# Layer 3 of a four-layer convolution kernel: a first copy in two parts, gate chains at other slots, scales of three tiles on VectorE

## The chip, the cores and the metric

The kernel runs as one program on one core of a Trainium2 chip. The metric is the device time of one execution in microseconds (us). A core has five engines that run side by side, each with its own queue, in order: TensorE (PE: matrix products; PEld is its weight load), VectorE (DVE), ScalarE (ACT), GpSimd (POOL) and SyncE (SP, which here only issues DMAs). An instruction whose inputs or buffers aren't ready waits, and all that stands behind it in its engine's queue waits too.

## The reference

The kernel computes four layers on x of 4 x 256 x 48 x 48 floats, each `x = x + layer(groupnorm(x))`: attention (layer 0), a gated multiplication (1), a non-local block with a batch norm (2), and layer 3, the one that is changed:

```python
x = x + _L3_conv_ref(_gn(x), attn_w1, attn_w2, refine_w, refine_b)
...
def _L3_conv_ref(x, attn_w1, attn_w2, refine_w, refine_b):
    p = jnp.mean(xw, axis=(2, 3))
    h = jax.nn.leaky_relu(p @ attn_w1.T, SLOPE)
    a = jax.nn.sigmoid(h @ attn_w2.T)
    y = xw * a[:, :, None, None]
    y = conv_general_dilated(y, refine_w, padding='SAME', feature_group_count=C)
    y = y + refine_b[None, :, None, None]
    mu, var = mean(y), mean(square(y - mu))       # per sample and channel
    return leaky_relu((y - mu) * rsqrt(var + EPS), SLOPE)
```

`_gn` is a group norm with 32 groups of 8 channels; `refine_w` is a 3 x 3 depthwise kernel, one per channel; SLOPE is 0.01.

## The kernel before

Layers 0 to 2 (and their long run of products) are left as they are by the change. Layer 3 takes the last 150 us. Its work is cut into 8 tiles: 4 samples (`n`) by 2 halves of the channels (`k`), a tile being 128 channels by 48 x 48 pixels. The last sample's tiles are 6 and 7. The order of the samples is `SEQ`.

**Making a tile's image.** Layer 2's last product and the batch norm are applied on the way: `w_product` (L1650, PE) makes a chunk, `grow` (L1712, DVE) scales it, adds x and writes it into a padded image `pad` of 50 x 50 (five buffers), `border` (L1721, L1724, POOL) fills the rim with the value that the group norm turns to zero, `square` (L1736, ACT) sums squares for the group norm.

**Shifted copies.** The depthwise convolution runs on PE. For each half image (26 padded rows of 50 columns) 32 channels at a time are copied into `shifted`, at up to four shifts, so that one product contracts over several taps: 12 pieces `(j, q)` of 32 partitions by `CL` = 1298 columns, in one of three buffers `sh`. `place` (L1748 to L1756) makes a copy by SP's DMA (L1750), ACT (L1752), POOL (L1754) or DVE (L1756). Of later tiles, 8 pieces go by SP (`spread_out`) and 4 by ACT and DVE (`keep_here`). The two halves of tile 0 have a list of their own in `spread_first`.

**The convolution.** A tile is 6 *slots*, 48 in all. A slot (`products`, L1883) is 8 rows of the output: 3 row offsets by 4 groups of 32 channels, 12 products. Two slots fill one PSUM tile `cv`, one of three *groups* `g` of 768 pixels. ACT evicts it into `x` with its sum (`evict`, L1895), and sums its squares (`square`, L1906).

**The gate chain.** The gate `a` and the group norm of a sample are folded into one scale per channel, `rsa`, which is only needed after the convolution. Each sample has a chain of eight steps, which run at the slots `GATE_AT`, counted from the first slot of the sample's first tile:

1. `total` (L1795 to L1798, POOL) -> `gn_sq`
2. `groups` (L1802, PE), the sum over groups of channels
3. `read` (L1806, ACT) and `inverse` (L1810, L184, L1814, POOL) -> `pm`
4. `first_layer` (L1819, PE) on `pm`
5. `hidden` (L1826, ACT)
6. `leaky` (L1831, DVE) -> `hl`
7. `second_layer` (L1836, PE) on `hl`
8. `gate` (L1843, ACT) and `scaled` (L1847 to L1852, POOL) -> `rsa`

**The end of a tile.** When all groups are evicted: `moments` (L1915 to L1922, six small operations), `scales` (L1940 to L1958, of which the reciprocal root, L184, is always on POOL), `shift` (L1964, L1966), then per group `scale` (L1972, ACT), `leak` (L1978, DVE), `gain` (L1983, DVE: adds the residual) and `store` (L2016, SP). Of the last tile the sums come from `stats` and `aggregate` (L1928, L1932, DVE) on PSUM itself. A group's residual can also be added by PE with the identity as weights: `keep_up` and `join` (L1998, with ACT's L2010 behind it). `judge` is a check on layer 0's sums, whose last step `compare` (L2042, DVE) writes one number that the host reads.

**The order.** Each engine's order is the order of the calls (`manual_schedule`). `put_tile`, `put_before` and `put_chain` enter the calls into `events` with a slot and a rank; the slots are run in order, and in a slot the calls go by rank, calls of one rank in the order in which they were entered (tile 5's before the last sample's chain, for one). The ranks, from first to last: FRONT, CONV, PRODUCT, GROW, MID, EVICT, SMALL, MOMENTS, SQUARE, SCALE, LAST, PLACE, STORE. Behind slot 47 stands a tail written out by hand.

Of the kernel before, what the change touches and what calls it, by code (L numbers as in the profile page):

```python
# [23 lines left out]
NSL = N // SL  # L24
# [54 lines left out]
def usual_path(  # L79
    tc, x, wqkv, wout, vecs, dww, thphi_w, thphi_b, g_w, g_b, W_w, attn_w1, attn_w2, refine_w, out  # L80
):
    nc = tc.nc
    B = x.shape[0]
# [113 lines left out]
    def hum(out, n):  # L197

        for _ in range(n):
            nc.tensor.matmul(out, lhsT=gmat, rhs=gmat, start=True, stop=True)  # L200
# [798 lines left out]
    def strips_pe(b, norm, res):  # L999
# [103 lines left out]
        while n < len(rounds):  # L1103
            add()
            u = rounds[n][0]
            if u in placed and seen >= placed[u] + SETTLED and clock["t"] not in taken:
                product(n)
                n += 1
                if n + 1 < len(rounds):
                    build(n + 1)  # L1110
            for _ in range(FILLS_AT_ONCE):
                if not left or not may_fill(left[0][0], n):
                    break
                v, c = left.pop(0)
                place(v, c)
                if c == 15:
                    placed[v] = seen
            seen += 1
            yield 1
# [385 lines left out]
    for b in range(B):  # L1505
# [12 lines left out]
        if b + 1 < B:  # L1518
# [8 lines left out]
            at = [s for s in range(n) if s in work or s % NG == AT_TOTAL]  # L1527
# [76 lines left out]
    w_all = ps_w.tile([P, 2, 512], F32, name="w3")  # L1604
# [6 lines left out]
    def g_tile():  # L1611

        return cv_last["ps"][:, 1, SL:]
# [12 lines left out]
    W2 = HW + 2  # L1626
    NG3 = NSL // 2
    GW = 2 * SL
    RS = SL // HW
    HB = HW // 2  # L1630
    CH = (HB + 2) * W2
    CL = CH - 2
    NPAD = 5
    pads = [lp.tile([P, W2 * W2], F32, tag=f"pad{i}", name=f"pad{i}") for i in range(NPAD)]
    shifted = [lp.tile([P, 4, CH], F32, tag=f"sh{i}", name=f"sh{i}") for i in range(3)]
# [106 lines left out]

    HELD = [96, 96, P, P]

    def place(i, h, j, q, how):
        to = shifted[(2 * i + h) % 3][32 * q : 32 * q + 32, j, :CL]
        c0 = h * HB * W2 + SHIFT[j, q]
        fr = pads[i % NPAD][32 * j : 32 * j + 32, c0 : c0 + CL]  # L1748
        if how == "sp":
            nc.sync.dma_start(to, fr)  # L1750
        elif how == "act":
            nc.scalar.copy(to, fr)  # L1752
        elif how == "pool":
            nc.gpsimd.tensor_copy(to, fr)  # L1754
        else:
            nc.vector.tensor_copy(to, fr)  # L1756
# [3 lines left out]
    def spread_out(i, h):  # L1760

        for j, q in AWAY:
            place(i, h, j, q, "sp")

    def keep_here(i, h, js, how):

        for j in js:
            place(i, h, j, j, how)

    def spread_first(h):  # L1770

        if h == 0:
            how = dict(zip(AWAY, ("sp", "sp", "sp", "sp", "sp", "sp", "dve", "pool")))
            how |= {(0, 0): "act", (1, 1): "act", (2, 2): "act", (3, 3): "pool"}
        else:
            how = dict.fromkeys(AWAY, "sp")
            how |= {(0, 0): "dve", (1, 1): "pool", (2, 2): "dve", (3, 3): "pool"}
        for (j, q), e in how.items():
            place(0, h, j, q, e)

    class Chain:

# [239 lines left out]
    def judge():  # L2022

        of = {}

        def lows():
            ok = lp.tile([P, 2, LW], F32, name="ok")
            nc.vector.tensor_scalar(ok[:, 0, :], lsum, SUM_HI, None, ALU.is_le)
            nc.vector.tensor_scalar(ok[:, 1, :], lmin, SUM_LO, None, ALU.is_ge)
            of["okm"] = lp.tile([P, 1], F32, name="okm")  # L2030
            nc.vector.tensor_reduce(of["okm"], ok, AX.XY, ALU.min)

        def count():
            of["ps"] = g_tile()[0:1, 0:1]
            nc.tensor.matmul(of["ps"], lhsT=of["okm"], rhs=ones[:, 0:1], start=True, stop=True)

        def read():
            of["n"] = lp.tile([1, 1], F32, name="sound_n")
            nc.scalar.copy(of["n"], of["ps"])

        def compare():
            nc.vector.tensor_scalar(sound, of["n"], P - 0.5, None, ALU.is_ge)  # L2042

        return [(0, MID, lows), (2, SMALL, count), (3, MOMENTS, read), (5, MID, compare)]

    GATE_AT = {
        0: (3, 5, 6, 9, 10, 11, 11, 12), B - 1: (-2, -1, 0, 3, 4, 5, 7, 8),
    }
    for n in range(1, B - 1):
        GATE_AT[n] = (-2, 1, 2, 5, 6, 7, 9, 10)  # L2050
    chains = [Chain(n) for n in range(B)]
    convs = [Conv(i) for i in range(len(TILES))]

# [5 lines left out]
    grow(0, L2C - 1, first[L2C - 1], [0])  # L2059
    grow(0, 0, first[0], [1])  # L2060
    spread_first(0)
    for c in range(1, L2C):
        grow(0, c, first[c], [1])
    centres()
    spread_first(1)
    for c in range(L2C):
        square(0, c)
# [7 lines left out]
    FRONT, CONV, PRODUCT, GROW, MID, EVICT, SMALL, MOMENTS, SQUARE = range(9)  # L2075
    SCALE, LAST, PLACE, STORE = range(9, 13)
    events = {}

    def at(t, rank, fn):
        events.setdefault(t, []).append((rank, fn))  # L2080
# [23 lines left out]
    def put_tile(i, t, cv, final):  # L2104
        for s in range(NSL):
            at(t + s, CONV, lambda s=s: cv.products(s))
        if final:
            for s in range(NSL - 1):
                at(t + s + 1, MOMENTS, lambda s=s: cv.stats(s))
            return  # L2110
        for g in range(NG3):
            at(t + 2 * g + 2, EVICT, lambda g=g: cv.evict(g))
            at(t + 2 * g + 3, SQUARE, lambda g=g: cv.square(g))
        at(t + 2, EVICT, cv.centre)
        soon = t + 2 * NSL == T
        t += 0 if soon else 1 if i == len(convs) - 3 else 3 if cv.k else 5 if t == 0 else 4
        if soon:
            at(t + 9, MOMENTS, lambda: cv.moments(nc.vector))
            at(t + 9, MOMENTS, lambda: cv.scales(nc.vector))
            at(t + 10, FRONT, lambda: cv.shift(nc.vector))  # L2120
            for g in range(NG3):
                at(t + 10, SCALE, lambda g=g: cv.scale(g))
            return
        at(t + 8, FRONT, lambda: cv.moments(nc.gpsimd))
        at(t + 8, MOMENTS, cv.scales)
        at(t + 8, LAST, cv.shift)
        for g in range(NG3):
            at(t + 9 + g, SCALE, lambda g=g: cv.scale(g))
            u = t + (10 if t == 5 else 11) + g
            at(u, LAST, lambda g=g: cv.leak(g))  # L2130
            at(u, LAST, lambda g=g: cv.gain(g))
            at(u + 1, STORE, lambda g=g: cv.store(g))
# [4 lines left out]
    T = len(convs) * NSL  # L2137
    for i, cv in enumerate(convs):
        t = i * NSL
        put_tile(i, t, cv, i == len(convs) - 1)  # L2140
        if i > 1:
            put_before(t, i)
        if i:
            for h in range(2):
                at(max(0, t - 6 + 3 * h), PLACE, lambda i=i, h=h: spread_out(i, h))
            for dt, h, js, how in HERE:
                at(t + dt, PLACE, lambda i=i, h=h, js=js, how=how: keep_here(i, h, js, how))
        if i % NK == 0:
            put_chain(t, chains[i // NK].steps())
        if i < NK:  # L2150
            at(t + 18, STORE, lambda k=cv.k: reload(k))
    put_chain(13, judge())
    for t in range(min(events), T):
        for _, fn in sorted(events.pop(t, ()), key=lambda job: job[0]):
            fn()
    cv = convs[-1]
    cv.stats(NSL - 1)
    cv.aggregate()
    cv.scales(nc.vector)
    was = convs[-2]  # L2160
    was.leak(0)
    cv.shift(nc.vector)
    for g in range(NG3):
        cv.scale(g, cv.ps[g])
    hum(w_all[:, 1, SL:], 12)
    was.keep_up(1, w_all)
    was.leak(1)
    was.join(1, w_all)
    was.keep_up(2, cv.ps[0])
    was.leak(2)  # L2170
    was.join(2, cv.ps[0])
    was.gain(0)
    was.store(0)
    was.store(1)
    for g in range(NG3 - 1):
        cv.leak(g)
        cv.gain(g)
        if g == 0:
            was.store(2)
        cv.store(g)  # L2180
    cv.leak(NG3 - 1)
    for h, eng in enumerate((nc.scalar, nc.sync)):
        cv.gain_half(NG3 - 1, h)
        eng.dma_start(
# [771 lines left out]
def kernel(tc, *args):  # L2956


    sound = usual_path(tc, *args)
    with tc.If(sound == 0):  # L2960
        general_path(tc, *args)
# [72 lines left out]
```

## Time and profile before

| what | value |
|---|---|
| median of 3 runs | 3460.08 us (3459.35 to 3461.13) |
| the profiled execution: its own time | 3461.47 us |
| the profiled execution: span, first to last instruction | 3459.7 us |
| granted TensorE clock, mean over the span | 0.996 |
| last 21.0 us (3438.70 to 3459.70), busy | PE 8.37, DVE 13.54, ACT 7.31, POOL 1.10 |
| convolution slots 36 to 47 (3412.10 to 3438.70), busy | PE 26.60 of 26.60, DVE 15.97, ACT 20.05, POOL 15.29 |
| the 25.43 us ahead of these (3386.67 to 3412.10), busy | PE 21.65, DVE 22.00, ACT 24.66, POOL 14.29 |

Times within the execution are counted from the span's start. In a row of a timeline the columns are the start, the busy time, the engine, the line, the operation with output and input tiles, its shape, the number of records merged into the row, and in brackets the idle time before it with the engine, tile and line (or DMA) that ended it. In the windows view a row gives a stretch, its length, the busy time and the instructions of PE, PEld, DVE, ACT and POOL, the granted clock (1.00 is full speed), the share of the DMA engines that were busy, and GB/s. The clock line of the page is in tenths, one digit for each of 40 equal slices of the span.

### The profile page before, as it was taken

To read this page: it belongs to the slowest core of one execution; us is meant where nothing else is said; L and a number is where in the kernel's file an instruction comes from. 1 tells how busy PE (TensorE), PEld (TensorE's weight loads), DVE (VectorE), ACT (ScalarE), POOL (GpSimd) and SP (SyncE) were. 2 spreads that over 40 slices of the span, in tenths; PEclk is the share of its full clock that TensorE was granted. 3 is DMA by queue.
4 is the path that set the end of the run, shared out by engine and by line. 5 is a ranking of instruction groups with operands and counts; after the bars stand their busy time and mean duration, and the time that the engine had idled before them with its cause. 6 is when DMAs were issued, how large, how long until landed. Compare 5 with 4: busy or idle time off the path is not lost. (4 is left out here: it accounts for less than half of the span.)

```text
span 3459.7 us, 88715 instructions
## 1 busy us (share of the span) xinstructions
PE 3397.6 (98%) x37678; PEld 1711.7 (49%) x37678; DVE 2540.6 (73%) x3298; ACT 2297.1 (66%) x3690; POOL 824.9 (24%) x734
## 2 busy tenths in 40 slices
PE   8999999999999999999999999999999999899988
PEld 5555545555545444545454445554544444445533
DVE  3455545568788788687888787878887878857777
ACT  5565556565886687557866875568758855444577
POOL 2433333320011011101110010111011105776434
PEclk9999999999999999999999999999999999999999
DMA  2211111111111111121111110111111110221067
GB/s 91 49 23 27 22 27 22 27 22 27 21 32 22 27 22 27 27 72 22 27 22 27 15 31 15 31 18 31 18 28 17 30 21 9 59 62 11 8 152 230
DMA packets 111590, 127.20 MB, mean 37 GB/s; under 512 B 42912, under 2 KB 101648, under 8 KB 110416
## 3 DMA queue, kind: packets, MB, share of 16 engines
q1 hardware_dynamic: 109936, 119.53, 17.1%
q8 instruction: 297, 4.87, 0.6%
q10 hardware_dynamic: 1248, 1.91, 0.2%
q14 instruction: 109, 0.89, 0.1%
HBM read 56.99 MB, written 11.80 MB: 20 GB/s over the span
## 5 line engine op out<-in xcount | busy, mean ns | idle before, releaser
L330 ACT ACTIVATE pt<-sc 128x768 f32<-128x768 f32 x1944 | 1473.4, 810 | 759.8 <-PE sc L324 753.3
L370 DVE TENSOR_TENSOR acc<-acc,pt 128x768 f32<-128x768 f32 x1368 | 1367.1, 999 | 145.5 <-ACT pt L330 51.8
L344 PE MATMUL av<-pt,v 64*64 64x384 f32 x13824 | 1274.9, 484 | 0.0
L324 PE MATMUL sc<-q,k 64*64 64x384 f32 x13824 | 1270.1, 482 | 0.5 <-ACT pt L330 0.5
L324 PEld LDWEIGHTS sc<-q,k 64*64 64x64 f32 x13824 | 525.4, 133 | 589.6 <-issue 556.5
L344 PEld LDWEIGHTS av<-pt,v 64*64 64x64 f32 x13824 | 518.2, 133 | 568.4 <-issue 521.5
L421 POOL TENSOR_TENSOR o<-o,rinv 128x384 f32<-128x384 f32 x95 | 120.3, 1267 | 1712.4 <-DMA rinv<-rinv 1702.4
L355 POOL TENSOR_TENSOR half<-pt 128x768 f32<-128x768 f32 x189 | 369.0, 1957 | 495.2 <-ACT pt L330 417.0
L739 DVE SCALAR_TENSOR_TENSOR x<-pj,bo,x 128x384 f32<-128x384 f32 x192 | 118.5, 617 | 346.3 <-ACT row L388 188.0
L951 ACT ACTIVATE prod<-pd,wt 128x256 f32<-128x256 f32 x486 | 340.7, 761 | 0.2
L370 DVE TENSOR_TENSOR acc<-acc,half 128x768 f32<-128x768 f32 x171 | 187.6, 1097 | 169.4 <-POOL half L355 168.2
L625 PE MATMUL pj<-xs,w 128*128 128x384 f32 (+1 forms) x720 | 275.4, 505 | 0.0
L625 PEld LDWEIGHTS pj<-xs,w 128*128 128x128 f32 x720 | 124.1, 189 | 127.9 <-ACT v L664 34.3
L974 DVE TENSOR_REDUCE prod<-prod 128x256 f32<-128x1280 f32 x114 | 168.7, 1480 | 0.9 <-ACT prod L951 0.9
L344 PE MATMUL av<-pt,qv 64*64 64x384 f32 x1728 | 169.0, 495 | 0.0
L324 PE MATMUL sc<-qv,kd 64*64 64x384 f32 x1728 | 165.3, 487 | 2.3 <-ACT pt L330 2.2
L723 PE MATMUL pj<-o,wo 128*128 128x384 f32 (+1 forms) x384 | 161.3, 502 | 1.1 <-DVE x L739 0.8
L364 DVE TENSOR_TENSOR acc<-pt 128x768 f32<-128x768 f32 x99 | 119.7, 1209 | 39.3 <-ACT pt L330 39.1
L659 PEld LDWEIGHTS pj<-w,xs 128*128 128x128 f32 x1080 | 134.4, 191 | 24.2 <-issue 1.2
L659 PE MATMUL pj<-w,xs 128*128 128x128 f32 x1080 | 134.9, 275 | 0.0
L417 POOL TENSOR_TENSOR o<-raw 128x384 f32<-128x384 f32 x95 | 120.8, 1271 | 45.9 <-ACT raw L413 44.7
L413 ACT COPY raw<-av 128x768 f32<-128x768 f32 x108 | 86.4, 800 | 48.3 <-PE av L344 47.8
(304 smaller groups left out, 2256.4 us busy)
## 6 DMA issues: line engine op xcount, KB each, us to landing
xs<-in_x_dram SPq DMA_DIRECT2D x90, 384.0 KB
sh<-pad SPq DMA_DIRECT2D x126, 162.2 KB
rinv<-rinv SPq DMA_DIRECT2D x208, 94.5 KB
out_dram<-x SPq DMA_DIRECT2D x23, 384.0 KB
w<-in_wqkv_dram SPq DMA_DIRECT2D x32, 192.0 KB
x<-in_x_dram SPq DMA_DIRECT2D x4, 1152.0 KB
x<-in_x_dram SPq DMA_DIRECT2D x9, 384.0 KB
rinv<-ls SPq DMA_DIRECT2D x208, 1.5 KB
```

Of the source, the lines that this page charges most:

```text
L324: nc.tensor.matmul(ps[c * D : (c + 1) * D, h, :SL], lhsT=u["of"]["k"][r, j0 : j0 + D], rhs=u["of"]["q"][r, u["qc"]], start=True, stop=True,)
L330: nc.scalar.activation(pt, ps[:, :, :SL], AF.Exp, scale=u["scale"])
L344: nc.tensor.matmul(u["av"][h * D : (h + 1) * D, half, :SL], lhsT=value(u, j, h)[r], rhs=pt[r, h, :], start=j == 0, stop=j == JB - 1,)
L355: nc.gpsimd.tensor_add(half, pts[0], pts[1])
L370: nc.vector.tensor_add(u["acc"], u["acc"], term)
L417: eng.tensor_add(u["sum"], u["raw"][:, 0, :], u["raw"][:, 1, :])
L421: eng.tensor_mul(o, o, u["rinv"])
L625: nc.tensor.matmul(ps[:, :n], lhsT=at["w"][:, k, t, :], rhs=xs[s][:, k, :n], start=k == 0, stop=k == NK - 1,)
L659: nc.tensor.matmul(ps[:, i * P : (i + 1) * P], lhsT=xs[s][:, k, i * P : (i + 1) * P], rhs=at["w"][:, k, 2, :], start=k == 0, stop=k == NK - 1,
L723: nc.tensor.matmul(ps[:, :n], lhsT=wo[:, p, k * P : (k + 1) * P], rhs=o["o"][:, :n], start=True, stop=True,)
L951: nc.scalar.activation(bufs[n % 3][:, :, min(n, 1) + i].rearrange("p (r c) -> p r c", c=AS), pd[:, PAD + dr : PAD + dr + AS, PAD + dc : PA ...
L974: nc.vector.tensor_reduce(to, bufs[n % 3][:, :, : min(n, 1) + len(taps)], AX.X, ALU.add)
```

## The change

1. The first half image of tile 0 is copied in two parts for all 12 pieces: the columns of the first 10 rows (`RS + 2`, 500 of 1298 columns, which slot 0 reads), then the rest. Each piece stays with its engine.
2. `compare` runs at slot 13 + 9, last of its slot, where it ran at 13 + 5.
3. The chains of the last two samples run at the slots (-2, 1, 2, 3, 4, 5, 5, 6). Before, the third sample (first slot 24) had (-2, 1, 2, 5, 6, 7, 9, 10), and the last one (first slot 36) (-2, -1, 0, 3, 4, 5, 7, 8).
4. Tiles 4, 5 and 6 get their moments, scales and shift on VectorE at `t + 8` (`t` is the tile's first slot); scales from `t + 9`, leaks and gains from `t + 11` (tile 6: two scales at `t + 9`, one at `t + 10`, leaks and gains from `t + 10`), each group's store a slot later. Before, tile 4 had them on GpSimd at `t + 12`, tile 5 at `t + 9`, and tile 6 on VectorE at `t + 9` and `t + 10` with its leaks, gains and stores in the tail.
5. In the tail only tile 7's first group is joined by PE; the two joins of tile 6 go, its last group's gain is on VectorE.

```diff
-    def place(i, h, j, q, how):
-        to = shifted[(2 * i + h) % 3][32 * q : 32 * q + 32, j, :CL]
+    def place(i, h, j, q, how, part=slice(0, CL)):
+        to = shifted[(2 * i + h) % 3][32 * q : 32 * q + 32, j, part]
         c0 = h * HB * W2 + SHIFT[j, q]
-        fr = pads[i % NPAD][32 * j : 32 * j + 32, c0 : c0 + CL]
+        fr = pads[i % NPAD][32 * j : 32 * j + 32, c0 + part.start : c0 + part.stop]
...
-        for (j, q), e in how.items():
-            place(0, h, j, q, e)
+        top = (RS + 2) * W2
+        for part in (slice(0, top), slice(top, CL)) if h == 0 else (slice(0, CL),):
+            for (j, q), e in how.items():
+                place(0, h, j, q, e, part)
...
-        return [(0, MID, lows), (2, SMALL, count), (3, MOMENTS, read), (5, MID, compare)]
+        return [(0, MID, lows), (2, SMALL, count), (3, MOMENTS, read), (9, LAST, compare)]
 
     GATE_AT = {
-        0: (3, 5, 6, 9, 10, 11, 11, 12), B - 1: (-2, -1, 0, 3, 4, 5, 7, 8),
+        0: (3, 5, 6, 9, 10, 11, 11, 12), B - 1: (-2, 1, 2, 3, 4, 5, 5, 6),
     }
     for n in range(1, B - 1):
         GATE_AT[n] = (-2, 1, 2, 5, 6, 7, 9, 10)
+    GATE_AT[B - 2] = GATE_AT[B - 1]
...
-        soon = t + 2 * NSL == T
-        t += 0 if soon else 1 if i == len(convs) - 3 else 3 if cv.k else 5 if t == 0 else 4
-        if soon:
-            at(t + 9, MOMENTS, lambda: cv.moments(nc.vector))
-            at(t + 9, MOMENTS, lambda: cv.scales(nc.vector))
-            at(t + 10, FRONT, lambda: cv.shift(nc.vector))
+        if i >= len(convs) - 4:
+            soon = i == len(convs) - 2
+            at(t + 8, MOMENTS, lambda: cv.moments(nc.vector))
+            at(t + 8, MOMENTS, lambda: cv.scales(nc.vector))
+            at(t + 8, LAST, lambda: cv.shift(nc.vector))
             for g in range(NG3):
-                at(t + 10, SCALE, lambda g=g: cv.scale(g))
+                at(t + 9 + g // (1 + soon), SCALE, lambda g=g: cv.scale(g))
+                u = t + 11 - soon + g
+                at(u, LAST, lambda g=g: cv.leak(g))
+                at(u, LAST, lambda g=g: cv.gain(g))
+                at(u + 1, STORE, lambda g=g: cv.store(g))
             return
+        t += 3 if cv.k else 5 if t == 0 else 4
...
-    was = convs[-2]
-    was.leak(0)
+    was.leak(NG3 - 1)
     cv.shift(nc.vector)
     for g in range(NG3):
         cv.scale(g, cv.ps[g])
     hum(w_all[:, 1, SL:], 12)
-    was.keep_up(1, w_all)
-    was.leak(1)
-    was.join(1, w_all)
-    was.keep_up(2, cv.ps[0])
-    was.leak(2)
-    was.join(2, cv.ps[0])
-    was.gain(0)
-    was.store(0)
-    was.store(1)
-    for g in range(NG3 - 1):
+    cv.keep_up(0, w_all)
+    was.gain(NG3 - 1)
+    was.store(NG3 - 2)
+    was.store(NG3 - 1)
+    for g in range(NG3):
         cv.leak(g)
-        cv.gain(g)
-        if g == 0:
-            was.store(2)
-        cv.store(g)
-    cv.leak(NG3 - 1)
+    cv.join(0, w_all)
+    cv.store(0)
+    cv.gain(1)
+    cv.store(1)
     for h, eng in enumerate((nc.scalar, nc.sync)):
         cv.gain_half(NG3 - 1, h)
```

More of the change, by code (lines that the diff above doesn't have):

```diff
@@ L2155, in usual_path @@
             fn()
-    cv = convs[-1]
+    cv, was = convs[-1], convs[-2]
     cv.stats(NSL - 1)
```

## The prediction

> **What bounds the kernel now.** I read the page first, then the timeline of single engines, then the granted clock of some stretches.
>
> ```profile
> span 3459.7 us, 88715 instructions
> PE 3397.6 (98%) x37678; PEld 1711.7 (49%) x37678; DVE 2540.6 (73%) x3298; ACT 2297.1 (66%) x3690; POOL 824.9 (24%) x734
> PEclk9999999999999999999999999999999999999999
> ```
>
> TensorE (PE) is busy 98% of the span, so a wait that PE is spared or given counts in full. All edits lie in the last 150 us (layer 3). There PE's timeline shows each wait in brackets; a slot of the convolution is 24 records of L1883 (12 f32 products, two records each) and lasts 2.0 us.
>
> ```profile
> 3311.25 0.80 PE L1883 MATMUL cv<-sh,taps 96*32 96x384 f32 x2 [1.03 <-DMA sh<-pad]
> 3312.69 4.43 PE L1883 MATMUL cv<-sh,taps 96*32 96x384 f32 x22 [0.64 <-DMA sh<-pad]
> ...
> 3386.67 6.01 PE L1883 MATMUL cv<-sh,taps 96*32 96x384 f32 x72
> 3392.61 0.39 PE L1819 MATMUL cv<-pm,w 128*64 128x1 f32 x4
> ...
> 3412.10 0.38 PE L1802 MATMUL cv<-gn_sq,gmat 128*128 128x2 f32 x2 [2.88 <-POOL gn_sq L1798]
> 3412.41 9.73 PE L1883 MATMUL cv<-sh,taps 96*32 96x384 f32 x96
> 3422.07 0.39 PE L1819 MATMUL cv<-pm,w 128*64 128x1 f32 x4
> 3422.40 7.95 PE L1883 MATMUL cv<-sh,taps 96*32 96x384 f32 x96
> ```
>
> Three waits stand there: 1.67 us for the first copies and 2.88 us at the last sample's L1802. Four slots after the latter took 9.73 us, four later ones 7.95: 1.78 us lost to the clock. The windows view has the granted clock in its last column but two (0.57; 0.50 in an earlier layer's stretch):
>
> ```profile
> 3412.00:3416.00 4.00, 3.90 (x26) 2.53 (x30) 2.49 (x3) 3.94 (x9) 2.74 (x7) 0.57 0.98 342
> 3173.60:3180.40 6.80, 6.53 (x42) 2.95 (x46) 2.57 (x10) 1.30 (x2) 1.40 (x1) 0.50 0.08 5
> ```
>
> The gate chain crosses all engines. What its L1819 waits for is `pm`, GpSimd's last step (L1814); VectorE (DVE), which the change loads more, has one hole in this part:
>
> ```profile
> 3391.16 0.95 POOL L1814 TENSOR_TENSOR pm<-dev,gn_rs 128x2 f32<-128x2 f32 x1
> 3410.30 4.27 DVE L1756 COPY sh<-pad 32x1298 f32<-32x1298 f32 x5
> 3421.85 0.96 DVE L1978 SCALAR_TENSOR_TENSOR x<-x 128x768 f32<-128x768 f32 x1 [7.27 <-ACT x L1972]
> ```
>
> **The change part by part.** Times are those of the profile of before.
>
> *First half image in two parts.* Twelve copies become 24 (SyncE 6 to 12 issues, ScalarE 3 to 6, DVE 1 to 2, GpSimd 2 to 4). SyncE issues every 0.64 us and a copy lands 2.6 to 3.1 us later, so the six first parts land about as early as the sixth whole one did or sooner, with 38% of the bytes (500 of 1298 columns). Slot 0 then has up to 1.67 us less to wait. But DVE runs without a gap to 3317.02 (L444) and idles only 0.97 us before the grow at 3317.99; PE's next product, L1650 at 3319.93, needs that grow's buffer. Hence no more than about 1.6 can be had. Twenty issues from 3306.89 end at 3319.0 and land near 3321.6, where slot 3 starts at 3322.0: just hidden, and a miss costs the same again. Bounds −2.1 (clock drop also shortened) and 0; I take −1.3.
>
> *Sound compare later.* One DVE instruction of 0.13 us, from slot 18 to slot 22, last of its slot. The 1.85 us that the waits view puts on it (L1650 at 3367.56) ends with the grow of 3366.37 to 3367.51, queued ahead of it. 0.
>
> *Sample three's chain (tiles 4 and 5).* L1802 and the read stay; L1819 moves from after slot 29 to after slot 27, L1836 from after 33 to after 29. PE reaches L1819 at 3386.67 + 1.98 = 3388.65. But `pm` is ready at 3392.11: ScalarE's read is at 3389.08, then GpSimd's 0.97, 0.72 and 0.95, and nothing makes them earlier. PE waits 3.5 (the two small-op prices on GpSimd, 0.2 and 0.95, allow 2.4). Slots 28 and 29 end near 3396.6; the hidden read (L1826) stands behind the eviction of 3396.46 to 3397.48, so L1831 follows at 3397.75, L1836 at 3397.85: a second wait of 1.25. Slot 30 starts at 3398.4 against 3392.93, 5.5 late. Behind L1831 on DVE stand tile 2's last leak and gain and the next grow; DVE loses that time too. Slots 30 to 35 end near 3413.2.
>
> *Last sample's groups (L1802), from after slot 35 to after slot 37.* `gn_sq` is ready at 3412.04, PE now gets there near 3417.3, so the wait of 2.88 is gone and so is its 1.78 of clock. With 5.5 lost and 4.7 won, PE ends slot 37 about where it did (3418.3 before), up to 0.9 sooner.
>
> *Moments, scales and shift of tiles 4 and 5 on DVE; last L1819.* The key step. Per tile, ten instructions leave GpSimd for DVE; only the reciprocal root (L184) stays, now in GpSimd's queue waiting for DVE's in_ve. Tile 5's root stands directly ahead of the last chain's L1810, L184 and L1814, all of one slot. So `pm`, which PE needs after slot 39 as before, now waits for everything ahead of tile 5's moments in DVE's queue. From the grow that follows PE's resumed slots (ends near 3408.25), with row durations (leak 0.96 + gain 1.02 = 1.97 a pair with gaps; copy 0.84): tile 4's moments 1.78 (3438.46 to 3440.24) to 3410.0; pair to 3412.0; shift 0.2 and two pairs to 3416.1; a copy to 3416.9; two of tile 4's pairs to 3420.8; two copies to 3422.5; its last pair to 3424.5; two copies to 3426.2; tile 5's moments to in_ve 1.45, 3427.65; then GpSimd 0.58 + 0.24 + 0.72 + 0.20 and gaps, 3429.9 (3430.4 if the clock drops in sample three's wait). PE stands there from about 3421.8: 8.1 us of wait. Against 3422.07 before: +8.3. DVE's 7.27-us hole before 3421.85 does not cover it: it lies behind those pairs in the row of before, and the 5.5 us lost at sample three have pushed them into it. Bounds +5 (no second wait there, small ops at their shortest) and +10.5 (leaks wait for ScalarE's scales as they did twice, 0.9 to 1.6 each).
>
> *Clock after that.* A wait of 2.88 cost 1.78. One of 8 costs at least this, and at most what the longest half-speed stretch shows (6.8 us at 0.50, so 3.4 lost). I take 2.5.
>
> [...]
>
> *Tail.* From L1819 to PE's end the slots are the same. Then, before, DVE went from the last product (3438.68) to the aggregate at 3442.28 and to the end of the last half gain at 3452.73. Now one join stays of two and tile 6 has its first leaks and gains behind it: after the last shift DVE has a gain 1.0, three leaks 2.86, a gain 1.0, halves 1.15 = 6.0 against 8.7 (3444.02 to 3452.73). −2.5 (bounds −3.5 and 0, if the leaks moved ahead delay the aggregate as much). Tile 7's first piece waits for PE and ScalarE beside that. The last three 384-KB pieces now leave nearly together, 1.0 us each at the 381 to 408 GB/s that the DMA view shows for the closing stores (3447 to 3455): a queue of 1.3 (0 to 2).
>
> Sum: −1.3 + 8.3 + 2.5 − 2.5 + 1.3 = +8.3. The span goes from 3459.7 to 3468.0, the profiled execution from 3461.47 to 3469.8. The median of the runs shown, 3460.08, lies 1.39 below that execution, so I predict 3468.4.
>
> **The rivals.** About 0.2% (7 us) is what a measurement of this kernel can tell from no change.
>
> A, the forecast: the last L1819 waits 6 to 9 us on DVE's queue. 3468.4; its own range 3464.5 to 3472.
>
> B, the same wait, but short: DVE works through its queue faster since PE's earlier pauses let ScalarE's scales arrive first, and the clock holds as in most 1-us waits of this layer. Wait 3 to 4 instead of 8.1, clock 1.7: −1.3 + 3.5 + 1.7 − 2.5 + 1.3 = +2.7, 3462.8. For it: the 7.27-us hole. Against: each item counted above is really queued ahead.
>
> C, the other side, faster: both samples' chains are served in time, since DVE's small ops (0.15 to 0.21 us) replace GpSimd's, which take 0.8 to 0.98 beside DVE. Then what remains is the start −1.3, the spared 2.88 and 1.78, and −1.2 in the tail: −7.2, 3452.9. It needs `pm` of the last sample before 3422 and of sample three before 3390; the row of L1814 at 3391.16 speaks against the second, the queue of pairs against the first. It decides once the wait at the last L1819 falls under about 1 us.
>
> D, worse: tile 4's three stores now stand ahead of tile 7's second-half copies in SyncE's queue and wait for DVE's late gains; a transfer of eight copies (1.3 MB) then starts late and slots 45 to 47 wait 3 to 4 us, and the clock also falls in sample three's wait (1.7, since 3.5 exceeds 2.88). 3468.4 + 4.6 = 3473.0. Against: the lag in which PE stands lets SyncE catch up.
>
> That the change does not do what it says: each moved instruction stands where the slots put it; I see nothing for it.
>
> **How the numbers follow.** A 0.62, B 0.17, C 0.11, D 0.10. The predicted time is A's, 3468.4. The range 3462.0 to 3473.0 holds A and nearly all of B, and about half of D; outside are C and half of D, with some of B. A and D are slower by over 0.2% (above 3467.0), except for A's lower end: 0.62 × 0.87 + 0.10 = 0.64, and with B's upper end 0.67. Within 0.2%: B and A's lower end, 0.22. Faster: C, 0.11.
>
> **What would show each step.** Start: the waits of 1.03 and 0.64 at the first two L1883 groups shrink, and the next L1650 starts before 3319.9. Sample three: L1819 shows 2.4 to 3.5 us from GpSimd's `pm`, L1836 1 to 2 us from DVE's `hl`. L1802 of the last sample has no wait. The last L1819 waits about 8 us on `pm`, and GpSimd's in_ri root before it on DVE's in_ve for as long; the granted clock is near 0.5 for some 3 us after. Tail: from PE's last product to the end 1 us or so less than 21. The prediction is wrong if the last L1819 waits under 3 us (then B or C), or if PE stands anywhere else for more than 2 us.

## The result and the profile after

| what | before | after |
|---|---|---|
| median of 12 runs | 3460.82 us (3458.87 to 3463.22) | 3468.75 us (3466.92 to 3472.84) |
| ratio of the times, 95% interval | | 1.0023, 1.0016 to 1.0031 |
| profiled execution, span | 3459.7 us | 3466.6 us |
| from layer 3's first weight product (L1650) to the end | 158.27 us | 166.16 us |

The change costs 7.9 us in the medians (3468.75 - 3460.82), against 8.3 forecast (3468.4). The two spans differ by 6.9 only, since the layers before, which are the same, took 1.0 us less in the profile after: layer 3's first group of weight products starts at 3300.44 there and at 3301.43 before. So below every profile is read from that product on: 166.16 - 158.27 = +7.89.

PE's timeline of the changed kernel, at the places that the prediction showed (lines have moved by two: L1885 is the convolution, L1804 groups, L1821 first_layer, L1838 second_layer):

```profile
3309.39 3.62 PE L1885 MATMUL cv<-sh,taps 96*32 96x384 f32 x24
3314.14 0.88 PE L1650 MATMUL w<-y,Ww 64*64 64x384 f32 x8 [1.13 <-DVE pad L1712]
...
3318.41 0.88 PE L1650 MATMUL w<-y,Ww 64*64 64x384 f32 x8 [1.32 <-DVE pad L1712]
...
3391.23 0.39 PE L1821 MATMUL cv<-pm,w 128*64 128x1 f32 x4 [3.33 <-POOL pm L1816]
3391.56 4.08 PE L1885 MATMUL cv<-sh,taps 96*32 96x384 f32 x48
3396.83 0.60 PE L1838 MATMUL cv<-hl,w 64*128 64x1 f32 x4 [1.20 <-DVE hl L1833]
...
3415.83 0.38 PE L1804 MATMUL cv<-gn_sq,gmat 128*128 128x2 f32 x2
3416.14 4.08 PE L1885 MATMUL cv<-sh,taps 96*32 96x384 f32 x48
3429.32 0.58 PE L1821 MATMUL cv<-pm,w 128*64 128x1 f32 x4 [9.10 <-POOL pm L1816]
3429.84 6.10 PE L1885 MATMUL cv<-sh,taps 96*32 96x384 f32 x48
```

The wait of 2.88 at groups is gone; 3.33, 1.20 and 9.10 us have come, and the two slots after the longest took 6.10 instead of 4.08. The windows view shows the clock there (0.50, last column but two):

```profile
3429.80:3433.00 3.20, 3.20 (x21) 1.01 (x25) 0.79 (x2) 3.16 (x5) 0.00 (x0) 0.50 0.30 67
```

A ledger by stages, from these rows and those before (each stage's length, after minus before):

| stage | before | after | difference |
|---|---|---|---|
| first weight product to the first groups | 28.12 | 28.21 | +0.1 |
| to slot 27 | 57.12 | 57.11 | 0.0 |
| slot 27 to slot 30 (the third sample's chain) | 6.26 | 11.60 | +5.3 |
| slot 30 to the last first_layer | 29.14 | 31.96 | +2.8 |
| from there to PE's end (the convolution's last product) | 16.61 | 18.82 | +2.2 |
| from there to the end | 21.02 | 18.46 | -2.6 |

GpSimd's timeline shows the last chain behind tile 5's root, and its long wait for VectorE's in_ve:

```profile
3426.71 0.57 POOL L184 TENSOR_TENSOR in_ri<-in_ve,mhalf 128x1 f32<-128x1 f32 x1 [13.60 <-DVE in_ve L1945]
3427.36 0.22 POOL L1812 TENSOR_SCALAR gn_gv<-gn_gv 128x2 f32<-128x2 f32 x1
3427.67 1.32 POOL L184 TENSOR_TENSOR gn_rs<-gn_gv,mhalf 128x2 f32<-128x2 f32 x1
3429.07 0.19 POOL L1816 TENSOR_TENSOR pm<-dev,gn_rs 128x2 f32<-128x2 f32 x1
```

But ScalarE's read of the chain's groups, which pm needs as well, was late too:

```profile
3411.17 1.03 ACT L1974 ACTIVATE x<-x,in_sf,in_sc 128x768 f32<-128x768 f32 x1 [2.72 <-DVE in_sf L1968]
...
3422.68 0.14 ACT L1808 COPY gn_gv<-cv 128x2 f32<-128x2 f32 x1
```

In the kernel before, the read stood ahead of tile 4's scales in ScalarE's queue; its row in ScalarE's timeline is

```profile
3415.94 0.15 ACT L1806 COPY gn_gv<-cv 128x2 f32<-128x2 f32 x1
```

and the first of these scales came behind it, at 3420.79. In the changed kernel it stands behind all three. PE reached first_layer at 3429.32 - 9.10 = 3420.2, so ScalarE alone, which had stood 2.72 us before a scale of tile 4, would have made it wait. How much of the 9.10 is whose was the first question for experiments.

### The profile page after: what moved, and what is told of

The parts are those of the page before. It is cut to its first block, busy times and chain, and to the rows that moved or that the text cites. A ratio compares the mean times of both kernels' runs of the same rounds, so it can differ in the third digit from the quotient of the medians.

```text
span 3466.6 us, 88713 instructions
## 1 busy us (share of the span) xinstructions
PE 3396.5 (98%) x37670; PEld 1706.3 (49%) x37670; DVE 2546.9 (73%) x3322; ACT 2296.6 (66%) x3692; POOL 816.6 (24%) x710
```

## The experiments

Each kernel was timed in 10 or 11 executions between executions of the kernel before on the same chip (before's median there: 3460.40 for root_behind, no_split, chain2_alone and chain3_alone, 3461.35 for chain3_old, pool_scales, tail_alone and groups_one_later, 3460.83 for the other four). Single executions of one kernel spread over 3 to 9 us, so differences under some 3 us are read from stages of the profiles and not from the medians. A profile is one execution of its kernel. Moments, scales and shift of tiles 4 and 5 on VectorE (part 4 of the change) and the later `compare` (part 2) have no run of their own.

**Tile 5's root behind the chain.** One rank later for tile 5's moments and scales (`late = SQUARE if i == len(convs) - 3 else MOMENTS`):

```diff
-            at(t + 8, MOMENTS, lambda: cv.moments(nc.vector))
-            at(t + 8, MOMENTS, lambda: cv.scales(nc.vector))
+            at(t + 8, late, lambda: cv.moments(nc.vector))
+            at(t + 8, late, lambda: cv.scales(nc.vector))
```

> The changed kernel, with tile 5's moments and scales entered one rank later (SQUARE), so that GpSimd's root of tile 5 stands behind the last chain's three steps and no longer ahead of them. Theory 1 (the queue order is all of it): the last first_layer product waits 0 to 1 us instead of 9.1, its clock loss of 2 goes too, the time falls by 9 to 11 us, to about 3459. Theory 2 (the order is half of it): in the profile of the changed kernel ScalarE's read of the chain's second step ends only at 3422.8, itself late since ScalarE stood 2.7 us before a scale of tile 4 that waits for VectorE's shift; pm can then be ready near 3424.2, PE waits about 4, and the time falls by 5 (4 to 6), to 3463.5. Rival: the wait moves on to second_layer, whose hl stands in VectorE's queue behind the same work: fall under 2, and a wait of 5 or more at second_layer.

Measured 3465.77 us, ratio to before 1.0016 (1.0006 to 1.0025). Its PE and GpSimd timelines:

```profile
3391.28 6.86 PE L1885 MATMUL cv<-sh,taps 96*32 96x384 f32 x48
...
3426.76 0.58 PE L1821 MATMUL cv<-pm,w 128*64 128x1 f32 x4 [5.32 <-POOL pm L1816]
3427.27 5.94 PE L1885 MATMUL cv<-sh,taps 96*32 96x384 f32 x48
```

```profile
3424.15 0.61 POOL L1812 TENSOR_SCALAR gn_gv<-gn_gv 128x2 f32<-128x2 f32 x1 [9.80 <-ACT gn_gv L1808]
3424.84 1.59 POOL L184 TENSOR_TENSOR gn_rs<-gn_gv,mhalf 128x2 f32<-128x2 f32 x1
3426.51 0.20 POOL L1816 TENSOR_TENSOR pm<-dev,gn_rs 128x2 f32<-128x2 f32 x1
```

Theory 2 holds: 9.10 becomes 5.32, now ended by ScalarE's read. The queue order is worth 3.8 us of the wait, and as much of the stretch from slot 30 to first_layer (28.15 us against 31.96). The medians fall by 3.0 (3468.75 to 3465.77; 2.6 when each is counted from its own before), less than the 4 to 6 that were expected: the wait is 5.32 and not 4, the loss behind it stays (5.94 against 4.08), and in this profile slots 28 and 29, behind the third sample's wait, lost their clock too (6.86 against 4.08, with a granted clock of 0.50 from 3391.5 to 3395.5), which made slot 30, counted from first_layer, 1.7 us later.

**The same work on GpSimd.** In the changed kernel `eng = nc.vector if soon else nc.gpsimd`, passed to moments, scales and shift.

> The changed kernel, with moments, scales and shift of tiles 4 and 5 on GpSimd at the same slots and ranks. Theory 1 (VectorE's queue is what tile 5's root waits for): GpSimd's moments need only ScalarE's sums, first_layer's wait falls from 9.1 to the 4 to 5 us that ScalarE's late read leaves (the experiment with the root behind), time 3 to 5 below the changed kernel. Theory 2 (tile 5's last squares, which ScalarE ends at 3423.8 in the changed kernel, after the chain's read, hold tile 5's moments on either engine): GpSimd's ten small operations then stand ahead of the chain's three, the wait stays at 8 to 9, time within 2 us of the changed kernel.

Measured 3468.58 us, ratio 1.0019 (1.0009 to 1.0028). GpSimd's timeline:

```profile
3422.89 0.50 POOL L1918 TENSOR_TENSOR in_mv<-in_mv,in_st 128x2 f32<-128x2 f32 x1 [2.15 <-ACT junk L1908]
...
3429.54 0.23 POOL L1812 TENSOR_SCALAR gn_gv<-gn_gv 128x2 f32<-128x2 f32 x1
```

first_layer waits 6.87, between the two theories, and no difference in time to the changed kernel is seen. On GpSimd the small work takes from 3422.89 to 3429.54, its first six operations there 0.50 to 0.94 us each, and the chain's steps come behind it. From slot 30 to first_layer this profile needs 29.70 us, the changed kernel 31.96 and root_behind 28.15: with the small work ahead of the chain, on either engine, the chain is later than with it behind.

**The last chain alone at the old slots.** In the changed kernel `B - 1: (-2, -1, 0, 3, 4, 5, 7, 8)`, `B - 2` as changed, and tile 6's moments one rank later, since rsa is made in their slot.

> The changed kernel, with the last sample's chain alone back at its old slots (groups after slot 35, read and inverse in slot 36, so ahead of tile 5's root in GpSimd's queue; first_layer after slot 39 as in both). Tile 6's moments stand one rank later, since rsa is now made in their slot. Theory (the new slots of this chain, not the lateness of VectorE as such, make the long wait): the 9.1 us wait and its 2 us of clock go; groups waits 1 to 1.5 us for gn_sq and may lose 1.8 to the clock again; time 6 to 9 us below the changed kernel, 3460 to 3463. Rival (the small work on VectorE makes the chain late wherever it stands): a wait of 4 us or more stays at first_layer or second_layer, time 0 to 4 below.

Measured 3466.60 us, ratio 1.0014 (1.0005 to 1.0024): 2 us below the changed kernel (2.7 when each is counted from its own before). The waits are the theory's (1.15 at groups, 2.01 at first_layer, 0.60 at second_layer), the time is not: 6 to 9 us were expected from them. PE ends 6.00 us earlier, counted from the first weight product (3442.32 - 3300.62 against 3448.14 - 3300.44), but from there to the end it is 21.1 again and not 18.5. VectorE's timeline shows it late there:

```profile
3433.30 0.15 DVE L1833 SCALAR_TENSOR_TENSOR hl<-hraw 64x1 f32<-64x1 f32 x1 [3.79 <-ACT hraw L1828]
...
3448.46 0.32 DVE L1934 BATCH_NORM_AGGREGATE in_mv<-in_bn 128x2 f32<-128x36 f32 x1
```

The aggregate comes 6.1 us after PE's end (3442.32), where the changed kernel needs 3.3 (3448.14 to 3451.39).

**The tail and tile 6 alone.** The kernel before with tile 6's block and the tail as in the change; tile 6's moments stand at rank SQUARE of `t + 8`.

> The kernel before, with tile 6's earlier moments, scales, leaks and gains and the new tail alone (tile 6's moments in slot 44 behind the chain's last step). Theory (the two profiles: from PE's last product to the end 21.0 us before, 18.5 after): 2 to 3 us faster than before. Rival (it only pays where PE's waits have given VectorE time to catch up; before, VectorE is 3.6 us behind PE at its end, and tile 6's leaks and gains, now ahead of the last stats, put it further behind): the aggregate comes 2 to 4 us later, time -1 to +2.

Measured 3462.85 us, ratio 1.0006 (0.9996 to 1.0015). The rival holds in its kind; in size the aggregate is later than its 2 to 4 us, and the 1.5 us in the medians aren't clear of noise. PE ends at 3438.17, the aggregate stands at

```profile
3446.21 0.32 DVE L1932 BATCH_NORM_AGGREGATE in_mv<-in_bn 128x2 f32<-128x36 f32 x1
```

8.0 us behind (3.6 in the kernel before), and the end 24.3 us behind instead of 21.0. The 2.6 us that the end gains in the changed kernel go with PE's waits, during which VectorE catches up:

```profile
3440.54 0.57 DVE L1930 BATCH_NORM_STATS2 in_bn<-cv 128x6 f32<-128x384 f32 x1 [4.34 <-PE cv L1885]
```

This row is the changed kernel's: VectorE stands 4.34 us for a product of PE, and ends that wait 7.6 us before PE's end. In tail_alone it never waits for PE behind hl. The other half of the comparison is in chain3_alone (below), which has a last wait of 6.92 us and the old tail. From its timelines of PE and VectorE:

```profile
3441.22 2.94 PE L200 MATMUL w<-gmat 128*128 128x128 f32 x24
```

```profile
3442.42 0.32 DVE L1932 BATCH_NORM_AGGREGATE in_mv<-in_bn 128x2 f32<-128x36 f32 x1
```

Its aggregate is 1.2 us behind PE's end, and its span ends at 3459.5, 18.28 behind. So with a long last wait the old tail takes 18.3 us and the new one 18.5 (16.9 to 18.5 in the five profiles that have it); without one they take 21.0 (kernel before) and 24.3 (tail_alone), and the new one 21.1 in chain3_old, whose wait is 2.0. The new tail isn't shown to gain anything in either state.

**The third sample's chain alone.** The kernel before with `GATE_AT[B - 2] = (-2, 1, 2, 3, 4, 5, 5, 6)`.

> The kernel before, with the third sample's chain alone at the new slots. Theory: first_layer waits 3.3 and second_layer 1.2 us as in the changed kernel, slot 30 starts 4.5 to 5.5 later; but the last sample's groups product, which waits 2.9 us for gn_sq and loses 1.8 to the clock in the kernel before, then comes to a gn_sq that is ready, so that nearly all is given back: time +0 to +2 us. Rival (gn_sq moves with PE, since it depends on the image that PE makes): the wait at the groups product stays, +4.5 to +6 us.

Measured 3464.21 us, ratio 1.0009 (0.9999 to 1.0019). Its PE timeline:

```profile
3392.63 0.59 PE L1819 MATMUL cv<-pm,w 128*64 128x1 f32 x4 [3.33 <-POOL pm L1814]
3393.15 6.94 PE L1883 MATMUL cv<-sh,taps 96*32 96x384 f32 x48
3400.02 0.60 PE L1836 MATMUL cv<-hl,w 64*128 64x1 f32 x4
...
3415.13 0.38 PE L1802 MATMUL cv<-gn_sq,gmat 128*128 128x2 f32 x2
3415.44 7.95 PE L1883 MATMUL cv<-sh,taps 96*32 96x384 f32 x96
```

As the theory had it, groups no longer waits and its clock loss is gone (7.95 for four slots against 9.73). But here the wait of 3.33 cost its clock (granted 0.58 and 0.57 in 3391.5 to 3399.5): two slots took 6.94 instead of 4.08, which swallows the second wait. Layer 3's stretch is 160.61 us, +2.3. In the medians it is +3.8, at the edge of the noise, above the theory's 0 to 2 and below the rival's 4.5 to 6.

**The last chain alone.** The kernel before with `B - 1: (-2, 1, 2, 3, 4, 5, 5, 6)`.

> The kernel before, with the last sample's chain alone at the new slots; tiles 4 and 5 stay on GpSimd as before. Theory (first_layer two slots after groups is too tight whatever the scales do, since the read stands in ScalarE's queue and GpSimd's moments of tile 4 stand ahead): the 2.9 us wait and the 1.8 of clock at groups go, a wait of 4 to 7 us at first_layer comes; time +0 to +3. Rival (only VectorE's queue makes first_layer late): first_layer waits under 1.5 us, and the time falls by 3 to 5 us.

Measured 3462.83 us, ratio 1.0007 (0.9997 to 1.0017). The theory holds: groups doesn't wait, first_layer does, though no small work of tiles 4 and 5 is on VectorE here:

```profile
3422.09 0.58 PE L1819 MATMUL cv<-pm,w 128*64 128x1 f32 x4 [6.92 <-POOL pm L1814]
3422.60 6.41 PE L1883 MATMUL cv<-sh,taps 96*32 96x384 f32 x48
```

ScalarE's read is at 3418.87, behind a scale of tile 4 for which ScalarE had stood 2.26 us, and GpSimd's three steps take 0.97, 1.36 and 0.44 (0.22, 0.72 and 0.20 in the kernel before). Two slots between groups and first_layer aren't enough here, whichever engine makes the scales.

**The first copy.** In the changed kernel whole again (`if False` in place of `if h == 0`), and in the kernel before in two parts alone.

> The changed kernel, with the first half image copied whole again. Theory (from the two profiles: 0.5 us won at the third weight product, 0.6 lost at slot 3 where copies of the second half land late): no change, within 1 us. Rival (the prediction's 1.3 us of gain is there and hidden in the noise of one profile): slower by 1.3 us or more, with the first two groups of the convolution waiting 1.0 and 0.6 again.

> The kernel before, with the first half image in two parts alone. Theory (0.86 us more of copies in VectorE's queue and late landings of the second half give back what slot 0 wins): within 1 us of before; from the first weight product to the first groups product 27.9 to 28.3 us, as before (28.1). Rival (the prediction): 1.3 us faster, with that stretch at 26.8.

Measured 3469.37 us, ratio 1.0024 (1.0015 to 1.0034), and 3461.06 us, ratio 1.0001 (0.9992 to 1.0010): nothing either way. From the first weight product to the first groups product the seven profiles in two parts took 27.6 to 28.2 us, the seven whole ones 26.4 to 28.2 (26.4 in the two in which the 22 records behind the first waits took 2.73 and 2.75 us; chain3_alone is one of them, with a granted clock of 1.00 there, against 0.71 in the kernel before). Slot 0 is indeed ready sooner (no wait at 3309.39 in the changed kernel), but the next products then wait for VectorE's grow, 1.13 and 1.32 us in the rows above. VectorE's row says why its queue is no earlier:

```profile
3305.73 1.69 DVE L1756 COPY sh<-pad 32x500 f32<-32x500 f32 x2
```

The row holds both parts (500 and 798 columns): 1.69 us where the whole piece took 0.83. Its cause stays open: GpSimd copies pieces beside it in both kernels; in the changed one GpSimd began first (3305.64 against 3305.73), in the kernel before VectorE did (3306.79 against 3306.82). Whether that order matters isn't shown, since no run has the split without GpSimd's copies. ScalarE needed 4.51 us for six parts against 3.87 for three pieces. And at slot 3 PE waits 0.6 us for copies of the second half image:

```profile
3322.09 0.20 PEld L1885 LDWEIGHTS cv<-sh,taps 96*32 96x32 f32 x6 [0.60 <-DMA sh<-pad]
```

**Less work on VectorE, two tries.** The changed kernel leaves out the leaks of tile 3 (`if i != 3:`), and chain3_old those of tile 5 (`if i != 5:`).

> The changed kernel, which leaves out the three leaky steps of tile 3 (2.9 us of VectorE, queued ahead of tile 5's moments and shift). Theory (VectorE's queue up to tile 5's shift sets both pm and, through ScalarE's scale, copies and read, what follows): the last first_layer waits 6.0 to 6.5 instead of 9.1 and the time falls by 2.5 to 3.5. Rival (it is ScalarE's read that holds pm, with or without VectorE): the wait stays above 8, time within 1 us of the changed kernel.

> The kernel chain3_old, which leaves out the three leaky steps of tile 5 (2.9 us of VectorE, behind the last leaky of the chain). Theory (in chain3_old VectorE works without a gap from hl to the aggregate, 6.1 us behind PE's end, so that the end is VectorE's): time 2 to 3 below chain3_old, the stretch from PE's last product to the end 18 to 19 instead of 21.1. Rival (the end belongs to PE and the stores): no change, within 1 us.

The first: 3469.07 us, ratio 1.0023 (1.0013 to 1.0032). Its profile shows a shorter wait,

```profile
3427.25 0.59 PE L1821 MATMUL cv<-pm,w 128*64 128x1 f32 x4 [7.00 <-POOL pm L1816]
```

2.1 us less, and the aggregate 2.8 us earlier (148.13 us behind the first weight product against 150.95). But the profiled execution, 3464.19, is one of the two quickest of ten; the others lie between 3467.2 and 3472.7, and the median doesn't fall. That VectorE's queue lengthens this wait is seen in one profile, that it lengthens the time isn't shown.

The second missed: 3467.20 us, ratio 1.0019 (1.0010 to 1.0028), no lower than chain3_old, and 20.8 us from PE's last product to the end. The gaps that the missing leaks leave are waits for ScalarE:

```profile
3437.63 1.02 DVE L1985 SCALAR_TENSOR_TENSOR x<-pad,bi,x 128x768 f32<-128x768 f32 x1 [1.72 <-ACT x L1974]
...
3439.53 0.57 DVE L1930 BATCH_NORM_STATS2 in_bn<-cv 128x6 f32<-128x384 f32 x1 [0.88 <-ACT ga L1845]
```

So a VectorE without gaps wasn't by itself the bound of chain3_old's end. As the rows of old_no_leak5 read, ScalarE and VectorE wait for each other in turn; no run tests this: tile 5's shift (3428.6), ScalarE's scale, two copies, an eviction and the hidden read (3433.26), VectorE's hl, ScalarE's gate read (3439.35), rsa, tile 6's scales (from 3442.42), their leaks, the aggregate.

**A version that might beat both.** The kernel before with the last sample's groups, read and inverse one slot later, `B - 1: (-2, 0, 1, 3, 4, 5, 7, 8)`, twice.

> The kernel before, with groups of the last sample one slot later (after slot 36), read and inverse in slot 37, the rest of its chain unchanged. Theory: the wait of 2.9 us at groups falls to about 1, its clock loss of 1.8 may go, pm is still there in time: 1 to 3 us faster than before. Rival (pm comes a slot later and first_layer waits what groups no longer does): no change, with 1.5 to 3 us of wait at first_layer.

> The kernel groups_one_later again, with more rounds, as the only version so far that was below the kernel before. Theory: 1 to 2 us faster than before, with the interval's upper end at or under 1. Rival: no difference that more rounds confirm, ratio within 0.0002 of 1.

3459.88 us, ratio 0.9996 (0.9986 to 1.0006), then 3461.05 us, ratio 1.0001 (0.9992 to 1.0010): no difference. As the rivals said, first_layer waits 2.69 us in both profiles, what groups no longer does. No kernel tried here is shown to beat the kernel before.

## Why the prediction was right, point by point

- **What bounds the kernel**: right as an account of the changed kernel, where all of the +7.9 is in waits of PE, their clock, and the tail. That a wait which PE is spared or given "counts in full" is not: chain3_old brings PE's end 6.0 us forward and the kernel's end only 3.4 in the profile (162.78 against 166.16 us) and 2 to 3 in the medians. In chain3_alone PE ends 3.3 us later than in the kernel before (140.57 against 137.25 us behind the first weight product), the kernel 0.6 (158.85 against 158.27). VectorE and ScalarE are close behind PE, and no experiment that took the waits away gave the 7.9 back.
- **Start, -1.3**: wrong, +0.1. The working counted DVE's copies (1 to 2) and did not price them; the second part cost VectorE 0.86 us, which is about the idle 0.97 from which the gain was to come (why it cost so much is open, as said above). "Just hidden, and a miss costs the same again" was a miss by 0.6 us. In the medians no_split and split_alone both say 0.
- **Sound compare, 0**: nothing seen of it; the stage up to slot 27 is the same to 0.01 us.
- **Third sample's chain**: 3.5 and 1.25 forecast, 3.33 and 1.20 measured, 5.5 late forecast, 5.34 measured. That the clock also falls there was in rival D and left out of A: it did in five of the seven profiles that have the 3.33-us wait, not in the changed kernel's own.
- **Groups**: right, no wait and 7.95 for four slots in chain2_alone.
- **Last first_layer, 8.1 us of wait, +8.3**: 9.10 and +8.2 (5.34 + 2.82). The sum over VectorE's queue was right as a time for pm, but not as a cause that could be taken away: with the root out of the way ScalarE's read still holds PE for 5.3 us, and chain3_alone has 6.9 us without any of VectorE's new work. The working left ScalarE's read out of the sum. The chain's new slots, which put the read behind one (chain3_alone) or all three scales of tile 4, make the wait, and the small work ahead of the chain lengthens it.
- **Clock, 2.5**: 2.2 from first_layer to PE's end. The 1.7 of rivals B and D, for waits of 3 to 4 us, is shown by no run: behind 3.33 us two slots took 2.6 to 2.9 us longer in five profiles and no longer in two, behind the last wait (5.3 to 9.1 us) 1.5 to 2.7 longer.
- **Tail, -2.5 + 1.3 = -1.2**: -2.6. The aggregate came 0.35 sooner behind PE, VectorE's run behind it took 7.70 instead of 10.45, and from the last half gain to the end it is 0.54 more, not 1.3 (7.51 against 6.97; it varies from 6.0 to 8.6 among the profiles). The size of VectorE's part was right, the reason for the gain was not. Measured against chain3_alone, which has the old tail and a long wait too, the run is shorter (7.70 against 10.47), but the aggregate is later by 2.05 (3.25 against 1.20), and the end is no sooner. That is the bound of 0 that the prediction gave for leaks that delay the aggregate as much; the 2.6 us go with the last wait. Alone, the same edits cost 1.5 us in the medians (not clear of noise), and 3.3 in the tail of the profile.
- **The sum**: +8.3 against +7.9; the 1.4 us of gain too much at the start and the 1.4 us of gain too little in the tail cancel. That the sum is this close is luck; that the waits at first_layer and the clock behind the last one make the loss is not. Rivals B and C needed a short last wait and did not come. Tile 7's copies, D's other half, show no wait behind slot 39.

GpSimd's prices differ with what VectorE does beside it. In the kernel before, the first eight of its small operations (L1915 to L1941) take 0.19 to 0.24 us each for tile 4 (from 3415.65 to 3417.85), while VectorE stands; for tile 5 the last four of them, beside VectorE's leaks and gains (from 3421.85), take 0.81 to 1.01. The chain's root takes 0.72 in the kernel before while VectorE stands (3419.47), and 1.41 in chain3_old beside a leak and a gain (3422.66). Why is not shown.

## What to carry to other kernels

Moving steps of a chain that crosses engines to earlier slots makes them earlier only where the slowest engine's queue has room: here ScalarE read the groups 6.5 us after PE had made them (3416.2 to 3422.7), and the slots taken out of the chain came back as waits of PE. Price each part against the state in which it will run: here the end came sooner behind PE because of a wait that another part of the change had made, and the new tail alone made it later. And a wait of the busiest engine isn't the kernel's time when two other engines are close behind it: in chain3_old PE ended 6.0 us sooner than in the changed kernel, the kernel 3.4. A copy cut in two cost ScalarE 1.17 times the whole piece (4.51 against 3.87 us), and VectorE, beside GpSimd's copies, twice (1.69 against 0.83).

## What had not been expected of the hardware

TensorE's clock fell after waits of quite different lengths, and not in every execution:

- after 3.33 us in five of seven profiles (a granted clock of 0.50 to 0.63 from 3391.5 to 3395.5 in these five, 1.00 in the two others);
- after waits of 1.03 and 0.64 us close together in some of the profiles with a whole first copy: the 22 records after them took 4.06 to 4.45 us, or 2.73 to 2.75 (granted clock 0.71 in the kernel before with 4.43, 1.00 in chain3_alone with 2.75);
- after the last wait in all six profiles in which it was 5.32 to 9.12 us: two slots took 5.61 to 6.76 us instead of 4.08 (granted clock 0.50 behind the 9.10 us of the changed kernel);
- by the times of four slots alone, after 2.69 us in one of two profiles (9.64 us, then 7.95) and after 2.04 in tail_alone (9.76), and not after 2.01 in chain3_old (7.95) and 2.02 in split_alone (8.07); nor, by two slots, after 2.07 in old_no_leak5 (4.08).

A fall cost 1.3 to 2.9 us. It is probably one reason why single executions of one kernel lie up to 9 us apart: in no_leak3 the two quickest had a mean granted clock of 0.996 and 0.997, the eight others 0.993 to 0.995.
